# Twenty-five tiles of gathered rows: fetched edge by edge by SyncE instead of by GpSimd

## The chip, the cores and the metric

The kernel runs on one core of a Trainium2 chip. The core has a matrix engine (TensorE, PE in the profile, with its weight loads listed apart as PEld), a vector engine (VectorE, DVE), an activation engine (ScalarE, ACT), a general engine that also issues indirect transfers (GpSimd, POOL), and SyncE (SP), which computes nothing and issues transfers. All of them work through their own list of instructions in order and wait for each other on semaphores. Sixteen DMA engines move the data between the chip's large memory (DRAM below) and the on-chip memory of 128 partitions.

The metric is device time in microseconds of one execution. A comparison takes medians of several executions, and runs of the kernel before made beside those of the kernel after.

## What is computed

A graph of 12,500 nodes and 212,500 edges, of which 12,500 are loops (a node to itself). Every node has 64 numbers. Two layers follow each other, both with a layer norm ahead and a sum onto the nodes at the end:

```python
h = relu(layernorm(x))
# layer 1: a 64x64 matrix for each of 16 edge types
msg = h[src] @ weight[type]
x = x + segment_sum(msg, dst)
h = relu(layernorm(x))
# layer 2: a small network on both ends and 8 attributes of the edge
m = relu(concat(h[src], h[dst], attr) @ W1 + b1) @ W2 + b2
x = x + segment_sum(m, dst)
```

The edges come sorted by dst. src is random, so h[src] is a gather of rows of 64 float32 (256 B) from all over a table.

## The kernel before

The host hands over the arrays with no arithmetic. On the chip the edges that are not loops (200,000 of them) are first compacted into a list edges_c, and then treated in 1563 tiles of 128 edges, in groups of G = 4 tiles, 391 groups for each layer. The list is made in eight parts (UPTO holds their first tiles); the codes and source numbers of part c+1 are computed while part c is worked on.

First layer (`first_layer`, L1249). Per group: `gather` (L1005) has GpSimd issue one indirect DMA for each tile, which lands the 128 rows of h_rows in a buffer `rows` (14 such buffers of a group each, pool `land`, L316). ScalarE builds one-hot codes `oh_r` of target and relation; `products` (L1276) multiplies, on PE, the rows with the codes into `pa`, two matmuls a tile; `add` adds `pa` to a running table on VectorE at a place read from a register. Beside this main line run generators that are advanced by a step with every tile: preparing the next part, compacting and transposing the edge attributes (`attrs`, `turns_of_attrs`, with tiles u_in and u_out), loading h and loop relations of the next block (b_h, b_rel), and finishing blocks of nodes (`finish`, `tail_of`), which ends in the tables a_rows (h times the first part of W1) and b_rows (h times the second part).

Second layer (`second_layer`, L1449). Per group g: GpSimd gathers the rows of a_rows as before; SyncE loads a window of 40 rows of b_rows (`b_win`, two halves, six buffers) from a place that it reads from `first_row` into a register; every fourth group it loads positions (`local_bc`) and attributes (`of_edges`), of which ScalarE makes one-hots. PE multiplies the window with the one-hots into `pz`; one to three groups later VectorE adds the gathered rows, z = pz + rows; ScalarE applies the relu (`hid`), VectorE builds a one-hot `oh`, PE sums over edges (`pa`), and VectorE adds that to `sums`. The landing buffer of group g is free when z has read it.

The order on each engine is the order in which the program writes its instructions: the wrapper `InOrder` (L331 to 348; every operation that goes through it has the line L340 in the profile) holds each engine to it. `windows` (L1027) loads n = RG = 8 numbers of a row on chip into registers of an engine; a place computed from a register goes into a transfer as `bass.ds(r, n)`. A source number of an edge becomes float in `codes` (L939), is transposed on PE and lands as an integer column of `src_c`, from which the gather takes its 128 row numbers:

```python
V.tensor_single_scalar(sf, low, float(N - 1), op=ALU.min)
...
P_.indirect_dma_start(out=t[:, i, :], out_offset=None, in_=table,
    in_offset=bass.IndirectOffsetOnAxis(ap=idx[:, k : k + 1], axis=0))
```

Of the kernel before, what the change touches and what calls it, by code (L numbers as in the profile page):

```python
# [52 lines left out]
P = 128  # L53
N = 12500
D = 64
# [18 lines left out]
G = 4  # L74
# [101 lines left out]


LEAST, MOST = bounds()
WE = W + EA
EARLY = 4  # L180
NBW = 6
# [28 lines left out]
def gnn_kernel(  # L210
# [11 lines left out]
    b_rows = dram.tile([NW, D], F32, name="b_rows")  # L222
    x_mid = dram.tile([NB * P, D], F32, name="x_mid")
    attr_c = dram.tile([EC * EA, 1], F32, name="attr_c")
    attr_l = dram.tile([NB * P * EL, 1], F32, name="attr_l")
    turned_c = dram.tile([NGC * G * EA, P], F32, name="turned_c")
    turned_l = dram.tile([NB * EL, P], F32, name="turned_l")
    src_e = dram.tile([EARLY * 2, 2 * P], I32, name="src_e")
# [84 lines left out]
    def in_order():  # L313
        with ExitStack() as c2:
# [70 lines left out]
            tables = [own.tile([P, RH, SN + AHEAD], F32, name=f"table{k}") for k in range(2)]  # L385
            src_c = own.tile([P, UPTO[-1]], I32, name="src_c")

            rsel = own.tile([P, RH], F32, name="rsel")
            G_.iota(rsel, pattern=[[2, RH]], base=0, channel_multiplier=0, allow_small_or_imprecise_dtypes=True)
            V.tensor_single_scalar(rsel[D:], rsel[D:], 1.0, op=ALU.add)  # L390
# [37 lines left out]
            def weights():  # L428
                for k in range(2):
                    Q_.dma_start(wrel[k * D : (k + 1) * D], w_rel[k::2].rearrange("r i o -> i r o"))  # L430
                    Q_.dma_start(w1ab[k * D : (k + 1) * D], w1[: 2 * D].rearrange("(k i) o -> i k o", k=2))
                    yield
                Q_.dma_start(b1_bc, b1.unsqueeze(0).to_broadcast([P, D]))
                Q_.dma_start(t_loop[N:, :].rearrange("n o -> o n"), none)
                Q_.dma_start(attr_l[N * EL :, :].rearrange("(n c) o -> n (c o)", c=EL), zero[: NB * P - N, :EL])
                for t in hid_l:
                    V_.memset(t[:, :, D:], 1.0)
                yield
                Q_.dma_start(w1c, w1[2 * D :])
# [161 lines left out]
            def loop_attrs(q, psA):  # L601
# [337 lines left out]
            def codes(c, q, row, psA, V, S, T, rest):  # L939
# [16 lines left out]
                V.tensor_single_scalar(low, word, SRC - 1, op=ALU.bitwise_and)  # L956
                V.tensor_single_scalar(rel, word, 14, op=ALU.logical_shift_right)
                yield
                V.tensor_single_scalar(sf, low, float(N - 1), op=ALU.min)
                V.tensor_single_scalar(even, rel, 1, op=ALU.bitwise_and)  # L960
                yield
                V.tensor_tensor(d, q[:n, :, :, 1], bc(first_d, 2, P, [n, 2, P]), op=ALU.subtract)
                V.tensor_tensor(most[:n], d[:, 0, P - 1 :], d[:, 1, P - 1 :], op=ALU.max)
# [38 lines left out]
                    yield  # L1002
                bank.append(1)

            def gather(table, idx, g, last, first=0):  # L1005
                t = land.tile([P, G, D], F32, name="rows")
                tiles = [i for i in range(G) if first <= g * G + i < last]
                for i in tiles:
                    k = g * G + i
                    P_.indirect_dma_start(  # L1010
                        out=t[:, i, :],
                        out_offset=None,
                        in_=table,
                        in_offset=bass.IndirectOffsetOnAxis(ap=idx[:, k : k + 1], axis=0),
                    )
                return t, tiles[-1] + 1
# [232 lines left out]
            def first_layer(psA, loops_0):  # L1249
# [24 lines left out]
                    return g >= RAWG and (g - SHIFT) * G + i < NOT  # L1274

                def products(g, i):  # L1276
                    for half in range(2):
                        T_.matmul(
                            pa_of[g][half * D : (half + 1) * D, i, :],
                            lhsT=rows_of[g][:, i, :],  # L1280
                            rhs=oh_of[g][:, i, half * HW : (half + 1) * HW],
                            start=True,
                            stop=True,
                        )
# [10 lines left out]
                        V_.tensor_tensor(to, to, pa_of[a][:, i, :].rearrange("p (r n) -> p r n", r=RH), op=ALU.add)  # L1295

                at = {}
                behind_ns = [0.0]
                for it in range(NG1 - RAWG + L1_ADD[1]):
                    g = it + RAWG  # L1300
                    if g < NG1:
                        k = (g - SHIFT) * G
                        if it == 0 or k in UPTO:
                            c = sum(k >= b for b in UPTO[1:])
                            for _ in coming:
                                next(fresh, None)
# [3 lines left out]
                        rows_of[g], n_of[g] = gather(h_rows[:, :], src_c, g - SHIFT, NTC, NOT)  # L1310
# [23 lines left out]
                    for j in range(max(len(now), len(adds))):  # L1334
                        for i in range(G):
# [11 lines left out]
                            if it >= BEGIN:  # L1347
# [101 lines left out]
            def second_layer(ps):  # L1449
# [39 lines left out]
                for h in range(2):  # L1489
                    one_hots(0, h)  # L1490
                of_z, of_hid, of_pe, of_add = (turns(lag, NGC) for lag in (L2_Z, L2_HID, L2_PE, L2_ADD))
                for it in range(NGC + L2_ADD[1]):

                    g = it
                    if g < NGC:
                        if g % RG == 0:
                            at_b.update(enumerate(windows(first_row, g, PAD_DST, Q_, min(RG, NGC - g)), g))
                        if g % RB == 0:
                            load_edges(g // RB + 1)
                        a_of[g], n_of[g] = gather((a_early if g < EARLY else a_rows)[:, :], src_c, g, NTC)  # L1500
                        n = n_of[g]
                        if n:
                            bw = b_win[g % NBW]
# [28 lines left out]
                    for g in of_z.get(it, []):  # L1532
                        n = n_of[g]
                        if n:
                            hid_of[g] = wk2.tile([P, G, D], F32, name="z", bufs=3)
                            z, a = (t.rearrange("p (j h) d -> p j h d", h=2) for t in (hid_of[g], a_of.pop(g)))
                            pz_g = pz_of.pop(g)
                            for j, h in ((slice(0, n // 2), slice(0, 2)), (slice(n // 2, n // 2 + 1), slice(0, n % 2))):
                                if n % 2 or h.stop == 2:
# [536 lines left out]
```

## Time and profile before

| | |
|---|---|
| median of 10 runs | 4832.84 us (4828.25 to 4835.29) |
| the profiled execution | 4832.1 us, its span 4830.2 us |
| granted clock of PE | 0.545 of full speed on average |
| GpSimd busy | 2992.2 us, 62% of the span, 3170 instructions |
| PE busy, weight loads busy | 2212.3 us and 1743.4 us, 14955 of each |
| ScalarE busy, VectorE busy | 1636.6 us and 1420.0 us |
| DMA, instructed by GpSimd | 101152 packets, 111.42 MB, 12.8% of 16 engines' span |
| DMA, instructed by SyncE | 454757 packets, 116.50 MB, 11.4% |

How to read it. The profile counts an engine as busy while one of its instructions works; waits, register instructions and the issue of a transfer are not counted for SyncE, so SyncE has no busy time at all and is read from its rows in the timeline. A group of instructions is shown as output<-inputs, the count, busy microseconds, mean nanoseconds of one, and the idle time ahead of them with what ended it; "issue" is idle time for which no wait was found. A view of stretches gives busy time and, in brackets, the number of instructions of an engine within each. In the timeline several like instructions in a row are merged, xN, and the second number is the time from the start of the first to the end of the last.

The chain of work that ended last is here mostly "issue" (37%) and an unknown queue (18%), so it says little about which engine bounds the kernel.

### The profile page before, as it was taken

The page shows a single profiled execution, that of the slowest core. Times are in us where ns is not written, and L with a number is a line of the kernel's source. Part 1 is how long each engine was busy: PE and PEld are TensorE (multiplying, and loading weights), DVE is VectorE, ACT ScalarE, POOL GpSimd, SP SyncE. Part 2 cuts the span into 40 slices and gives each one's busy share as a digit, 9 for nine tenths or more (in the row PEclk, how much of TensorE's full clock was granted, in tenths as well). Part 3 has the DMA queues.
Part 4 walks back from the last instruction along what each step waited for, and adds up shares of the span by engine and source line. Part 5 has one row for each costly group of instructions (what it writes and reads, how often), then busy time and mean ns, then how long its engine had stood idle before and what let it go on. Part 6 is the DMA issues. An engine that isn't in the chain of part 4 may idle for free.

```text
span 4830.2 us, 53034 instructions
## 1 busy us (share of the span) xinstructions
PE 2212.3 (46%) x14955; PEld 1743.4 (36%) x14955; DVE 1420.0 (29%) x4924; ACT 1636.6 (34%) x3341; POOL 2992.2 (62%) x3170
## 2 busy tenths in 40 slices
PE   0334444455543445455445444444444444444445
PEld 0223333333332333333334444444434443444434
DVE  5375564463552333223221111111111111111112
ACT  3444444444443444444432222222222222222222
POOL 5566666666665666666646666666666666666663
PEclk9755555555555555555555555555555555555555
DMA  3222322313323233222211112212121212122111
GB/s 92 54 62 46 67 62 43 68 40 78 67 48 63 49 52 50 45 46 46 47 42 39 41 41 42 43 40 43 40 43 41 43 41 42 41 42 43 40 39 30
DMA packets 569509, 234.60 MB, mean 49 GB/s; under 512 B 455824, under 2 KB 497680, under 8 KB 568950
## 3 DMA queue, kind: packets, MB, share of 16 engines
q0 software_dynamic: 101152, 111.42, 12.8%
q1 hardware_dynamic: 454757, 116.50, 11.4%
q10 hardware_dynamic: 13298, 3.20, 0.3%
q8 instruction: 123, 2.02, 0.2%
q14 instruction: 179, 1.47, 0.1%
HBM read 195.55 MB, written 35.25 MB: 48 GB/s over the span
## 4 chain that ended last, share of the span: by engine, by line
issue 37%; PE 21%; another core or an unknown queue 18%; DVE 7%; ACT 6%; POOL 4%; DMA 2%; DVEq 1%; SPq 1%; ACTq 0%; POOLq 0%
PE pa L340 10%; PE pz L340 5%; POOL rows L340 4%; ACT off_r L340 3%; PE pT L340 2%; DVE table L340 2%; PE po L340 2%; PE hT L340 1%; ACT off L340 1%; DVE z L340 1%; DVE k_a L340 1%; ACT oh_r L340 1%; SPq L340 1%; PE pab L340 1%
## 5 line engine op out<-in xcount | busy, mean ns | idle before, releaser
L340 POOL DMA_INDIRECT rows<-h_rows,src_c x1533 | 1461.9, 954 | 857.7 <-issue 401.8
L340 POOL DMA_INDIRECT rows<-a_rows,src_c x1547 | 1463.8, 946 | 841.0 <-issue 401.8
L340 PE MATMUL pa<-oh_r,rows 128*64 128x96 f32 x6132 | 778.5, 355 | 812.6 <-issue 600.1
L340 PEld LDWEIGHTS pa<-oh_r,rows 128*64 128x64 f32 x6132 | 558.7, 207 | 1044.4 <-issue 952.8
L340 ACT ACTIVATE hid<-z 128x256 f32<-128x256 f32 x391 | 159.8, 411 | 1685.1 <-DVE z L340 1261.3
L340 PE MATMUL pz<-b_win,of_edges 48*128 48x64 f32 x3126 | 497.8, 419 | 409.1 <-issue 366.9
L340 PE MATMUL pa<-oh,hid 128*65 128x40 f32 x3126 | 473.4, 304 | 408.4 <-issue 360.4
L340 DVE TENSOR_TENSOR table<-table,pa 128x96 f32 x1565 | 394.8, 252 | 892.9 <-remote 668.8
L340 PEld LDWEIGHTS pz<-b_win,of_edges 48*128 48x128 f32 x3126 | 425.8, 316 | 488.0 <-issue 428.7
L340 ACT ACTIVATE off_r<-iota_s,code 128x192 bf16<-128x192 f32 x1535 | 570.0, 444 | 0.0
L340 PEld LDWEIGHTS pa<-oh,hid 128*65 128x65 f32 x3126 | 396.6, 221 | 450.1 <-issue 377.8
L340 DVE TENSOR_TENSOR z<-pz,rows 128x256 f32<-128x256 f32 x392 | 164.4, 420 | 1088.0 <-issue 626.7
L340 ACT ACTIVATE oh_r<-off_r 128x768 f32<-128x768 bf16 x392 | 330.3, 843 | 381.1 <-remote 323.4
L340 DVE TENSOR_TENSOR sums<-sums,pa 65x40 f32 x391 | 73.0, 187 | 616.5 <-remote 391.0
L340 PE MATMUL pT<-table,wrel 128*64 128x256 f32 (+1 forms) x800 | 228.4, 579 | 41.8 <-issue 39.9
L340 ACT ACTIVATE off<-local_bc,neg_w 40x1024 bf16<-40x1024 bf16 x196 | 222.5, 1135 | 5.1 <-DMA local_bc<-dst_l 2.4
L340 ACT ACTIVATE of_edges<-off 40x1024 f32<-40x1024 bf16 x196 | 206.2, 1052 | 6.3
L340 DVE SCALAR_TENSOR_TENSOR table<-b_rel,rsel,hT 128x256 f32<-128x256 f32 (+1 forms) x400 | 169.1, 470 | 125.0 <-remote 76.3
L340 DVE COPY_PREDICATED k_a<-move,k_a 128x1712 int32<-128x1712 int32 (+8 forms) x124 | 186.3, 1503 | 2.1 <-issue 0.2
L340 PE MATMUL hT<-ident,b_h 128*64 128x128 f32 x392 | 54.6, 428 | 228.9 <-DVE table L340 79.9
L340 PE MATMUL po<-w2b,sums 65*128 65x64 f32 x196 | 54.0, 329 | 211.6 <-issue 208.3
L340 PE MATMUL po<-w1c,o_at 8*128 8x64 f32 x196 | 56.0, 335 | 194.4 <-issue 180.8
(242 smaller groups left out, 1547.9 us busy)
## 6 DMA issues: line engine op xcount, KB each, us to landing
rows<-a_rows,src_c POOLq DMA_INDIRECT x1547
rows<-h_rows,src_c POOLq DMA_INDIRECT x1533
local_bc<-dst_l SPq DMA_DIRECT2D x194, 80.0 KB
b_win<-b_rows SPq DMA_DIRECT2D x782, 10.0 KB
k_a<-in_attr_k SPq DMA_DIRECT2D x72, 144.0 KB
k_a<-in_attr SPq DMA_DIRECT2D x52, 132.0 KB
u_in<-attr_c SPq DMA_DIRECT2D x97, 64.0 KB
turned_c<-u_out SPq DMA_DIRECT2D x97, 64.0 KB
```

The costliest lines, as they stand in the source:

```text
L340: last_ins[self.engine] = getattr(self.engine, name)(*args, **kw)
```

## The change

Of the tiles, 25 are no longer gathered by GpSimd: the last of four tiles in 14 groups of the first layer (ROWS_1) and in 11 groups of the second (ROWS_2). The source numbers of these tiles are kept as integers and written as rows of a small tile `row_src`, one row of 128 numbers for each. A generator `one_by_one` has SyncE read eight of them at a time into registers and issue one DMA of a single row for each edge, 128 for a tile, into one of two buffers `by_row`; a buffer is used again when the product or the sum that reads it has been written down in the program. In the first layer the generator is advanced one or two steps with each tile (six in a group), in the second four steps in a group, so that a tile takes 22 and 33 groups. `gather` leaves the tile out, `products` and z take the rows from `by_row` instead; z of such a group is made in three instructions.

With it go some smaller edits: the register loads of the second layer read four places at a time and not eight (for SyncE's window of b_rows and VectorE's place in sums), the source numbers are clipped as integers and converted by an instruction of their own, and the table attr_l is longer by 60 rows, with the limit of a store moved to match.

```diff
+ROWS_1 = [UPTO[c] // G + k for c in range(1, PARTS) for k in (25, 47) if UPTO[c] // G + k < NGC - 1]
+ROWS_2 = list(range(40, NGC - 8, 33))
+ROWS = [g * G + G - 1 for g in ROWS_1 + ROWS_2]
...
-    attr_l = dram.tile([NB * P * EL, 1], F32, name="attr_l")
+    attr_l = dram.tile([(NB * P + KLN) * EL, 1], F32, name="attr_l")
...
+            row_src = own.tile([len(ROWS), P], I32, name="row_src")
+            by_row = [own.tile([P, D], F32, name=f"by_row{k}") for k in range(2)]
+            known = set()
...
-                Q_.dma_start(attr_l[N * EL :, :].rearrange("(n c) o -> n (c o)", c=EL), zero[: NB * P - N, :EL])
+                Q_.dma_start(attr_l[N * EL :, :].rearrange("(n c) o -> n (c o)", c=EL), zero[: NB * P + KLN - N, :EL])
...
-                V_.tensor_single_scalar(to, firsts, float(NB * P - KLN), op=ALU.min)
+                V_.tensor_single_scalar(to, firsts, float(NB * P), op=ALU.min)
...
-                V.tensor_single_scalar(sf, low, float(N - 1), op=ALU.min)
+                V.tensor_single_scalar(low, low, float(N - 1), op=ALU.min)
+                V.tensor_copy(sf, low)
                 V.tensor_single_scalar(even, rel, 1, op=ALU.bitwise_and)
+                for m, k in enumerate(ROWS):
+                    if b0 <= k < b0 + nt:
+                        r, i = divmod(k - b0, 2)
+                        (Q_ if c else nc.sync).dma_start(row_src[m : m + 1, :], low[r : r + 1, i, :])
+                        known.add(m)
...
+            def one_by_one(table, of, at):
+                for m in range(at, at + len(of)):
+                    while m not in known or (m - at >= 2 and of[m - at - 2] not in used):
+                        yield
+                    t = by_row[m % 2]
+                    for e0 in range(0, P, RG):
+                        for e, r in enumerate(windows(row_src[m : m + 1], e0, N - 1, Q_), e0):
+                            Q_.dma_start(t[e : e + 1, :], table[bass.ds(r, 1), :])
+                            yield
+                    fetched[of[m - at]] = t
+                    yield
...
-            def gather(table, idx, g, last, first=0):
+            def gather(table, idx, g, last, first=0, but=()):
...
-                for i in tiles:
+                for i in tiles[: G - 1] if g in but else tiles:
...
                 def products(g, i):
+                    r = rows_of[g][:, i, :]
+                    if i == G - 1 and g >= RAWG and g - SHIFT in ROWS_1:
+                        while g - SHIFT not in fetched:
+                            next(by_rows)
+                        r = fetched.pop(g - SHIFT)
+                        used.add(g - SHIFT)
...
-                            lhsT=rows_of[g][:, i, :],
+                            lhsT=r,
...
+                by_rows = one_by_one(h_rows, ROWS_1, 0)
...
+                            if it >= BEGIN:
+                                for _ in range(1 + i % 2):
+                                    next(by_rows, None)
...
+                used.clear()
+                by_rows = one_by_one(a_rows, ROWS_2, len(ROWS_1))
...
+                    if g >= 6:
+                        for _ in range(G):
+                            next(by_rows, None)
...
-                        if g % RG == 0:
-                            at_b.update(enumerate(windows(first_row, g, PAD_DST, Q_, min(RG, NGC - g)), g))
+                        if g % RB == 0:
+                            at_b.update(enumerate(windows(first_row, g, PAD_DST, Q_, min(RB, NGC - g)), g))
...
+                            m = n - 1 if g in ROWS_2 else n
...
+                            if g in ROWS_2:
+                                assert n == G
+                                V_.tensor_tensor(z[:, 1, 1, :], pz_g[:, 1, 1, :], fetched.pop(g), op=ALU.add)
+                                used.add(g)
...
-                            if g % RG == 0:
-                                at.update(enumerate(windows(place_row, g, SN + AHEAD2 - W, V_, min(RG, NGC - g)), g))
+                            if g % RB == 0:
+                                at.update(enumerate(windows(place_row, g, SN + AHEAD2 - W, V_, min(RB, NGC - g)), g))
```

More of the change, by code (lines that the diff above doesn't have):

```diff
@@ L1003, in take @@
                 bank.append(1)
-            def gather(table, idx, g, last, first=0):
+            def one_by_one(table, of, at):
[9 more added lines that the diff above has]
+                    yield
+            fetched, used = {}, set()
+            def gather(table, idx, g, last, first=0, but=()):
                 t = land.tile([P, G, D], F32, name="rows")
                 tiles = [i for i in range(G) if first <= g * G + i < last]
-                for i in tiles:
+                for i in tiles[: G - 1] if g in but else tiles:
                     k = g * G + i
@@ L1309, in first_layer @@
                             coming = beside_part(c, psA)
-                        rows_of[g], n_of[g] = gather(h_rows[:, :], src_c, g - SHIFT, NTC, NOT)
+                        rows_of[g], n_of[g] = gather(h_rows[:, :], src_c, g - SHIFT, NTC, NOT, ROWS_1)
                     for g in of_oh.get(it, []):
@@ L1491, in second_layer @@
                 of_z, of_hid, of_pe, of_add = (turns(lag, NGC) for lag in (L2_Z, L2_HID, L2_PE, L2_ADD))
+                used.clear()
+                by_rows = one_by_one(a_rows, ROWS_2, len(ROWS_1))
                 for it in range(NGC + L2_ADD[1]):
                     g = it
+                    if g >= 6:
+                        for _ in range(G):
+                            next(by_rows, None)
                     if g < NGC:
-                        if g % RG == 0:
-                            at_b.update(enumerate(windows(first_row, g, PAD_DST, Q_, min(RG, NGC - g)), g))
+                        if g % RB == 0:
+                            at_b.update(enumerate(windows(first_row, g, PAD_DST, Q_, min(RB, NGC - g)), g))
                         if g % RB == 0:
                             load_edges(g // RB + 1)
-                        a_of[g], n_of[g] = gather((a_early if g < EARLY else a_rows)[:, :], src_c, g, NTC)
+                        a_of[g], n_of[g] = gather((a_early if g < EARLY else a_rows)[:, :], src_c, g, NTC, 0, ROWS_2)
                         n = n_of[g]
@@ L1537, in second_layer @@
                             pz_g = pz_of.pop(g)
-                            for j, h in ((slice(0, n // 2), slice(0, 2)), (slice(n // 2, n // 2 + 1), slice(0, n % 2))):
-                                if n % 2 or h.stop == 2:
+                            m = n - 1 if g in ROWS_2 else n
+                            for j, h in ((slice(0, m // 2), slice(0, 2)), (slice(m // 2, m // 2 + 1), slice(0, m % 2))):
+                                if m % 2 or h.stop == 2:
                                     V_.tensor_tensor(*(t[:, j, h, :] for t in (z, pz_g, a)), op=ALU.add)
+                            if g in ROWS_2:
+                                assert n == G
+                                V_.tensor_tensor(z[:, 1, 1, :], pz_g[:, 1, 1, :], fetched.pop(g), op=ALU.add)
+                                used.add(g)
                     for g in of_hid.get(it, []):
```

## The prediction

> **What bounds the kernel now.** I read the page's busy line and its costliest groups first, then GpSimd's waits, then stretches of the timeline in the second layer, and last SyncE's own rows, because SyncE is the engine that takes the work over.
>
> The page: GpSimd is the busiest engine, and nearly all of it are two groups of gathers, 1533 from h_rows and 1547 from a_rows (16 more read a_early).
>
> ```profile
> PE 2212.3 (46%) x14955; PEld 1743.4 (36%) x14955; DVE 1420.0 (29%) x4924; ACT 1636.6 (34%) x3341; POOL 2992.2 (62%) x3170
> ...
> L340 POOL DMA_INDIRECT rows<-h_rows,src_c x1533 | 1461.9, 954 | 857.7 <-issue 401.8
> L340 POOL DMA_INDIRECT rows<-a_rows,src_c x1547 | 1463.8, 946 | 841.0 <-issue 401.8
> ```
>
> One gather is 0.95 us and 0.30 us of gap, 1.25 us. By the list of instructions by tile the first layer's gathers run from 82.5 to 2418 us and the second's from 2455 to 4779, so one gather passes in 2335/1533 = 1.52 us and in 2324/1563 = 1.49 us. The quarter of a microsecond above 1.25 is waiting. GpSimd's waits from 2600 to 4600 us say for whom:
>
> ```profile
> POOL rows L340 <- issue: 352.1, 1153, 0.6
> POOL rows L340 <- DVE oh L340: 330.2, 83, 4.3
> ```
>
> Every 4 groups, 4.0 us long, GpSimd waits until VectorE's z has freed a landing buffer 14 groups back. So GpSimd is not alone the bound; the consumers hold it. But the consumers are fast when GpSimd is quiet. The busy time in six stretches, PE's weight loads alone (columns: stretch and length, busy us and count, granted clock, DMA share, GB/s):
>
> ```profile
> 3502.00:3514.60 12.60, 1.70 (x6) 0.50 0.23 42
> 3514.60:3522.60 8.00, 6.83 (x56) 0.50 0.29 67
> 3522.60:3538.40 15.80, 2.46 (x12) 0.50 0.16 30
> 3538.40:3546.60 8.20, 7.07 (x60) 0.50 0.20 44
> ...
> 4779.50:4824.00 44.50, 29.09 (x222) 0.50 0.07 17
> ```
>
> GpSimd is idle from 3511.6 to 3515.6. In the 8 us from just before its restart PE gets 56 weight loads through, in the 15.8 us after them 12, one step of about 0.7 us at a time, until GpSimd has again stood still for some 2 us. The clock is 0.50 throughout. After the last gather (4779) PE stays quick and a group passes in about 3.2 us against 5.94 before. So while gathers run without a break PE falls into a slow stretch, which ends only when GpSimd is held up. SyncE falls into it with PE, as its timeline shows:
>
> ```profile
> 3540.48 1.75 SPq L340 DMA_DIRECT2D b_win<-b_rows  x4
> ...
> 3516.19 10.05 SPq L340 DMA_DIRECT2D b_win<-b_rows  x8
> ...
> 4800.11 3.92 SPq L340 DMA_DIRECT2D b_win<-b_rows  x8
> ```
>
> These are DMAs from a place held in a register, the form that the change adds: 0.44 and 0.49 us each in a quick stretch, 1.26 us on average in the ten microseconds where a slow stretch begins. It is not all waiting for data: the register move ahead of each takes 29 ns in the median and up to 1395 ns (instructions of b_win).
>
> ```profile
> L340 SPq MOVE b_win<-b_rows x782: 2/29/1395, 2480.6 to 4803.7; - x196
> ...
> L1029 SPq TENSOR_LOAD <-first_row x49: 762/784/1193, 2479.6 to 4785.1; - x49
> ```
>
> **What the change removes.** 25 gathers on GpSimd, 14 and 11. At 1.25 us (GpSimd alone) that is 31 us, at the pace at which gathers really pass 14 x 1.52 + 11 x 1.49 = 38 us. I take 38: one gather less lets GpSimd stop sooner, and the slow stretch end sooner.
>
> **What it adds on SyncE.** 25 x 128 = 3200 DMAs of 256 B and 25 x 16 = 400 loads of eight registers. In quick stretches: 0.50 us a DMA and 0.79/8 = 0.10 us of load, 0.60 us an edge, 77 us a tile, 1920 us in all. In slow stretches the price lies between 1.26 and 2.1 us (register step, move and DMA, each 0.7); I take 1.5 us, nearer the measured average, a third of the quick speed. A one-row transfer from a register's place is not in this trace: the nearest are b_win's 40 rows (0.50 us with its register steps) and the one-row load of place_row (0.70 us, no register); I take b_win's, the same form, and 0.70 would fill the first layer to 5.5 of 6.0 us. They stand in SyncE's queue in front of everything that it issues later: in the first layer h and relations for the next block, u_in, x_mid, a_rows, b_rows; in the second b_win, edges and one-hot places, which PE needs.
>
> First layer, 6.0 us a group, 6 edges in each: 3.6 us, beside what SyncE issues now: by the list of DMA issues u_in, turned_c, b_rel, b_h, x_b, x_mid, a_early, a_rows, b_rows and k_a, 704 at 0.40 us = 282 us over 389 groups, 0.7 us. Sum 4.3 of 6.0. Second layer, 5.94 us, 4 edges: 2.4 us, beside 782 b_win x 0.50 + 583 others x 0.32 + 98 loads x 0.79 = 655 us, 1.7 us a group. Sum 4.1 of 5.94. If SyncE were always quick, all of it would be hidden, and the 38 us gained.
>
> It isn't always quick. Second layer, a cycle of 4 groups, 23.7 us, of which 8.2 are quick: needed 4 x 4.1 = 16.4 us of quick work, to be had 8.2 + 15.5/3 = 13.4. Short 3.0 us. SyncE then gets later from cycle to cycle, b_win comes late, z after it, GpSimd waits longer, and that wait is quick time: a microsecond more of idle gives itself, and puts the next slow stretch off by some 1.6 us (idle 4.0 us here, next onset some 6.5 us after the restart, on average over the cycles from 3000 to 3500 us), worth 1 + 1.6 x 2/3 = 2.1 us. So the cycle grows by about 1.4 us; the 11 tiles are fetched over 11 x 33 groups, 91 cycles: +130 us. First layer, 2 groups, 11.8 us: around 1840 us GpSimd stands still 2.1 us in each and PE is quick for some 4.2 us (its weight loads, over the cycles from 1800 to 2000 us). Needed 8.6, to be had 4.2 + 7.6/3 = 6.7, short 1.9, an idle microsecond worth 1.9: +1.0 us for each of 14 x 22/2 = 154 pairs: +150 us.
>
> Ends of this term: nothing at all (quick stretches suffice, the 38 us stand), and SyncE's work done in quick time only: an idle of I gives I less the 2.2 us until PE is quick again, and 1.6 I after it, so (I - 2.2) + 1.6 I = 16.4, I = 7.2, 3.2 us more than now x 91 = 290 us, and in the first layer (0.9 us and 1.4) (I - 0.9) + 1.4 I = 8.6, I = 4.0, 1.9 us x 154 = 290 us, together 580. I take 280, between them, since SyncE does move in slow stretches.
>
> **Small edits.** Where SyncE begins a buffer again it waits for the product or sum that read it last, 23 times; behind it stand b_win or h loads that are issued 3 to 6 groups ahead, so nothing. The second layer's register loads are of 4, not 8: 49 more at 0.79 us on SyncE (counted in the 1.7) and 49 more on VectorE at 0.6 us = 29 us, and 11 z in three pieces instead of one, some 0.5 us each: VectorE is idle 85% of that layer, hidden except where z is what GpSimd waits for, at most 10 us. A conversion more in codes, 7 at 0.3 us, one more small DMA a fetched tile, 25 at 0.7 us, and a somewhat larger fill of zeros: in VectorE's and SyncE's slack.
>
> **A rule against it.** The trace: SyncE's register DMAs follow each other at 0.44 us, and their waits for earlier b_win DMAs are 39 us in all, 1.5 us at the longest. The Trainium skill, "DMA: Bandwidth & Descriptors", section "Rules for kernel authors", says that many small transfers should be joined into a large one and that under 64 KB one pays mostly overhead; the section "Anatomy of one DMA" puts about 2.0 us of fixed time on each (its fit is for GpSimd's). At 2.0 us one after the other the 3200 would be 6400 us, an estimate from that page; the spacing of 0.44 us shows that they overlap, so the issue price is the one to use.
>
> **Sum.** The profiled execution took 4832.1 us (span 4830.2 and 1.9 around it), 0.7 us under the median of 4832.84. 4832 - 38 + 280 = about 5075 us.
>
> **Rivals.**
> 1. It does what it says, faster: 4833 - 38 = 4795. For it: 4.3 of 6.0 and 4.1 of 5.94 us in quick time, SyncE now waits for others for half of the first layer (494 us for ACT's u_out from 300 to 2300 us), and buffers let it run ahead. It decides as long as SyncE's price per edge stays below about 0.9 us on average, where 6 edges and 0.7 us fill a group of the first layer. Against it: 15 of 23.7 us are slow.
> 2. SyncE gets hardly anything done in slow stretches, or its 10,000 more instructions (three a DMA, and the loads) and 3200 landings lengthen them: 4795 + 580 = 5375, beyond if the slow stretches grow. Against: counted in the trace from 3000 to 3500 us, quick parts with some 21 SyncE instructions last 7.2 to 8.3 us and those with some 30 last 8.1 to 9.4; more instructions did not end them sooner.
> 3. Gain and loss cancel: 4833. It needs a loss of 38 us, about 0.15 us in each of the 245 cycles and pairs.
>
> **Chances.** The forecast (SyncE late, 4880 to 5280) 0.52; rival 2 with more than that 0.21; rival 1, with smaller losses included, 0.20; rival 3 0.07. What a measurement of this kernel can tell from no change is about 0.2%, 10 us. So faster 0.20, same 0.06, slower 0.74. The range goes from the full gain, 4793, to the end of the forecast's term, 5375; what lies outside is the worse half of rival 2. The forecast's own range is 4880 to 5280.
>
> **What would show it.** 3055 gathers instead of 3080, the same 0.95 us each. by_row DMAs on SyncE at 0.45 to 0.5 us in quick and above 1.2 us in slow stretches, SyncE without long waits while they run. GpSimd's waits for VectorE longer than 4.0 us per cycle in the second layer, and than 2.1 us in the first; groups longer while tiles are fetched and as before in the last 20 groups, where nothing is. Wrong it would be if slow stretches last as long with SyncE never late (rival 1), or if a landing, not the issue, holds SyncE.

## The result and the profile after

The kernel after took 5304.5 us (median of 8 runs, 5289.92 to 5313.61), the kernel before beside it 4833.0 us. The ratio is 1.0973, 95% interval 1.0963 to 1.0982: 471 us slower, where 242 slower was forecast and 5280 us was the upper end of the forecast's own range. The profiled execution of the kernel after took 5300.15 us, its span is 5298.3.

The experiments were run on three chips, and the kernel before itself took other times there: about 3967 us on two of them, 4789 and 4838 us on the third. Each comparison below is with the kernel before, run beside it on the same chip. I call a chip late or prompt by that time, since it decides the sign of the result: on a prompt chip the change makes the kernel 0.8% faster. Which chip the first result came from isn't on record; its 4833 us make it a late one. The third chip was late both times, the other two were met once each, so whether lateness is a chip's own or a condition that it was in is not shown.

The page of the kernel after, on the late chip of the first result (columns: busy us and mean ns of one, then idle us before them and what ended most of it):

```profile
PE 2183.1 (41%) x14955; PEld 1751.7 (33%) x14955; DVE 1422.2 (27%) x4954; ACT 1643.7 (31%) x3341; POOL 2954.1 (56%) x3145
...
L343 POOL DMA_INDIRECT rows<-h_rows,src_c x1519 | 1438.6, 947 | 1086.9 <-issue 391.7
L343 POOL DMA_INDIRECT rows<-a_rows,src_c x1536 | 1449.1, 943 | 1065.1 <-DVE oh L343 571.8
L343 PE MATMUL pz<-b_win,of_edges 48*128 48x64 f32 x3126 | 623.6, 433 | 1296.8 <-DMA b_win<-b_rows 989.7
```

The gathers are 25 fewer and each as long as before. What grew is the idle time ahead of them, and ahead of `pz` the wait for `b_win`, a load that SyncE issues. By the list of instructions by tile the first layer's gathers now run from 82.1 to 2677.1 us and the second's from 2713.7 to 5247.6: 259.5 and 209.4 us longer than before, together 468.9 us, where the span grew by 468.1. GpSimd's waits from 2800 to 4800 us, as long a stretch of the second layer as the one shown of before (columns: us in all, times, longest):

```profile
POOL rows L343 <- DVE oh L343: 469.4, 135, 7.7
POOL rows L343 <- issue: 312.3, 1024, 0.3
POOL rows L343 <- DVE z L343: 66.1, 15, 15.0
```

The wait for VectorE grew from 330.2 to 469.4 us and is now up to 7.7 us long instead of 4.3. PE's weight loads from 3400 to 3600 us and after the last gather, kernel after (columns: stretch and length, busy us and count, granted clock, DMA share, GB/s):

```profile
3400.00:3600.00 200.00, 81.00 (x544) 0.50 0.18 38
5247.60:5292.00 44.40, 29.12 (x222) 0.50 0.07 17
```

Before, the same 200 us held 598:

```profile
3400.00:3600.00 200.00, 83.02 (x598) 0.50 0.20 42
```

The clock and the tail after the last gather (222 loads, 29.1 us, in both) are unchanged. SyncE's rows come from the list of instructions of `by_row`, then that of `row_src` (columns: count, shortest/median/longest ns, first and last start), and then its timeline from 1000 to 1012 us (columns: start, length, and how many in a row):

```profile
L343 SPq MOVE by_row<-h_rows x1792: 1/29/1408, 303.8 to 2595.2; - x200
L343 SPq DMA_DIRECT2D by_row<-h_rows x1792: 1/228/2542, 304.1 to 2596.0; - x200
```

```profile
L1056 SPq TENSOR_LOAD <-row_src x400: 1/709/3331, 302.9 to 5112.6; - x134
```

```profile
1000.06 11.96 SPq L343 DMA_DIRECT2D by_row<-h_rows  x11
```

A register move takes 29 ns in the median and up to 1408. Eleven edges in a row take 11.96 us, and that is hardly waiting for others: SyncE's longest sum of waits for one cause is 34.3 us in the whole span, where before it waited 531.8 us for ScalarE's `u_out` alone. The row of before, then that of the kernel after (columns: us in all, times, longest):

```profile
SPq L340 <- ACT u_out L340: 531.8, 62, 61.0
```

```profile
SPq L343 <- DMA by_row<-h_rows: 34.3, 71, 1.3
```

Two measures taken from the instruction rows serve for all runs below. The price of an edge is the time from the start of SyncE's DMA ahead of it to the start of its own, distances of 8 us or more left out. In the kernel after it is 1.02 us in the first layer and 1.04 us in the second on average: half of the edges (52 and 53%) are under 0.75 us, with a mean of 0.46, and the other half have a mean of 1.61 and 1.71 us. Nearly every edge with a register load ahead of it, one in eight, is in that other half; on a prompt chip all of these are above 0.75 us too, 1.43 and 1.34 us on average. Of the edges without a load 41 and 40% are above 0.75 us here, with the same means of 1.61 and 1.71, and on a prompt chip 8 and 1%. A late step is a distance of 0.67 to 0.745 us between the starts of two successive instructions of one engine, counted over 1800 us of the second layer (1600 on a prompt chip): SyncE of the kernel before has 642 among 2847 instructions.

### The profile page after: what moved, and what is told of

It is laid out like the page before. It is cut to its first block, busy times and chain, and to the rows that moved or that the text cites. A ratio compares the mean times of both kernels' runs of the same rounds, so it can differ in the third digit from the quotient of the medians.

```text
span 5298.3 us, 63235 instructions
## 1 busy us (share of the span) xinstructions
PE 2183.1 (41%) x14955; PEld 1751.7 (33%) x14955; DVE 1422.2 (27%) x4954; ACT 1643.7 (31%) x3341; POOL 2954.1 (56%) x3145
## 3 DMA queue, kind: packets, MB, share of 16 engines
q1 hardware_dynamic: 462019, 117.35, 10.5%
## 5 line engine op out<-in xcount | busy, mean ns | idle before, releaser
L343 POOL DMA_INDIRECT rows<-h_rows,src_c x1519 | 1438.6, 947 | 1086.9 <-issue 391.7
L343 PE MATMUL pz<-b_win,of_edges 48*128 48x64 f32 x3126 | 623.6, 433 | 1296.8 <-DMA b_win<-b_rows 989.7
L343 PE MATMUL pa<-oh_r,rows 128*64 128x96 f32 x6076 | 667.1, 351 | 844.8 <-issue 461.5
L343 PEld LDWEIGHTS pz<-b_win,of_edges 48*128 48x128 f32 x3126 | 519.6, 315 | 1398.6 <-DMA b_win<-b_rows 920.0
L343 PEld LDWEIGHTS pa<-oh_r,rows 128*64 128x64 f32 x6076 | 513.1, 207 | 1012.4 <-issue 867.7
L343 PE MATMUL pa<-oh,hid 128*65 128x40 f32 x3126 | 430.7, 311 | 57.7 <-issue 30.2
L343 ACT ACTIVATE oh_r<-off_r 128x768 f32<-128x768 bf16 x392 | 330.2, 842 | 252.3 <-remote 196.9
L343 PEld LDWEIGHTS pa<-oh,hid 128*65 128x65 f32 x3126 | 373.5, 226 | 104.0 <-issue 31.8
L343 DVE TENSOR_TENSOR z<-pz,rows 128x256 f32<-128x256 f32 (+2 forms) x403 | 164.4, 411 | 744.5 <-PE pz L343 419.6
L343 PE MATMUL hT<-ident,u_in 128*128 128x128 f32 (+3 forms) x107 | 44.5, 416 | 334.9 <-DMA u_in<-attr_c 131.4
L343 ACT COPY table<-table 128x1024 f32<-128x1024 f32 x49 | 51.2, 1045 | 306.3 <-DVE table L343 236.1
```

Of the source, the lines that this page charges most:

```text
L343: last_ins[self.engine] = getattr(self.engine, name)(*args, **kw)
```

## Experiments

**The first four runs met a chip without late steps.** There the kernel before takes 3967.83 us. The first run leaves the 25 gathers out, the second keeps them all and fetches the rows beside them unread, the third puts constants in place of the register, the fourth gives the work to ScalarE.

```diff
 # a_no_fetch
-                        while g - SHIFT not in fetched:
-                            next(by_rows)
-                        r = fetched.pop(g - SHIFT)
+                        r = rows_of[g][:, G - 2, :]
...
-                by_rows = one_by_one(h_rows, ROWS_1, 0)
+                by_rows = iter(())
...
 # b_fetch_beside
-                for i in tiles[: G - 1] if g in but else tiles:
+                for i in tiles:
...
-                        r = fetched.pop(g - SHIFT)
+                        fetched.pop(g - SHIFT)
...
 # c_constant
-                        for e, r in enumerate(windows(row_src[m : m + 1], e0, N - 1, Q_), e0):
-                            Q_.dma_start(t[e : e + 1, :], table[bass.ds(r, 1), :])
+                        for e, r in enumerate([(97 * (m * P + e)) % N for e in range(e0, e0 + RG)], e0):
+                            Q_.dma_start(t[e : e + 1, :], table[r : r + 1, :])
 # d_act
-                        for e, r in enumerate(windows(row_src[m : m + 1], e0, N - 1, Q_), e0):
-                            Q_.dma_start(t[e : e + 1, :], table[bass.ds(r, 1), :])
+                        for e, r in enumerate(windows(row_src[m : m + 1], e0, N - 1, S_), e0):
+                            S_.dma_start(t[e : e + 1, :], table[bass.ds(r, 1), :])
```

> The kernel after without the 3200 fetches: the 25 gathers are left out and nothing takes their place; products and z of those tiles use the rows of the tile before, so the values of 25 of 3126 tiles are not computed from their own rows. It measures the gain by itself. Theory (one gather less lets GpSimd stop sooner): 38 us less than before, 4785 to 4805. Rival (the consumers hold GpSimd, so a gather less is only a longer wait): 4833, as before.

> The kernel after with all 3105 of before's gathers in these two loops kept as well: SyncE fetches the 25 tiles beside them and nobody reads what it fetches. Theory (SyncE's own time makes b_win, u_in and the rest late): as slow as the kernel after plus the gathers, 5300 to 5345. Rival (the loss comes from PE and VectorE waiting for rows that arrive late): about 4835 to 4870.

> The kernel after with constant sources in place of registers (a fixed row for every edge, so these 25 tiles get the wrong rows): the same 3200 DMAs of one row, but one instruction on SyncE instead of three, and no register loads. Theory (SyncE's instruction time): an edge costs about 0.33 us quick and 0.7 us slow instead of 0.60 and 1.5 to 2.1; the second layer's cycle then needs 16 x 0.33 + 6.8 = 12.1 us of quick work where 13.4 are to be had, so most of the loss goes: 4795 to 4900. Rival (the landings or the transfers of 3200 small DMAs hold it): 5200 to 5300.

> The kernel after with the 400 register loads and 3200 DMAs issued by ScalarE instead of SyncE, at the same places of the program. Theory (PE and SyncE have slow stretches, ScalarE does not: its out DMA took 0.38 us in the middle of one, its activations their usual time): second layer ScalarE is busy 25% of the time and gets 2.4 us more of each 5.94, it fits and gains 16 us; first layer it is busy 43% and gets 3.6 us more of each 6.0, full, so up to 100 us lost there: 4800 to 4930. Rival (a slow stretch strikes whatever engine issues many instructions, or the DMAs themselves are the cost): 5150 to 5350.

Measured, with the ratio to the kernel before: a_no_fetch 3936.04 us, 0.9921 (0.9904 to 0.9938); b_fetch_beside 3968.19, 1.000 (0.999 to 1.001); c_constant 3936.37, 0.9921 (0.9905 to 0.9938); d_act 3953.87, 0.9966 (0.9951 to 0.998). So 25 gathers are worth 31.8 us there, 1.27 us each, and 3200 fetches on SyncE cost nothing that can be measured. On ScalarE they take back 18 us; in its trace a store of GpSimd waits 15.1 us for a landing of `by_row`, and 395 us of ScalarE's idle time ahead of `off_r` are put down to such landings; which of these makes the 18 us is not shown. These runs did not test what makes the first result slow, because what I took for its cause is missing: in the trace of b_fetch_beside SyncE has 4 late steps, its register moves for `by_row` never exceed 39 ns, and GpSimd waits more than 0.5 us only five times.

**The change again, and more loads for each edge.** These runs met a late chip, kernel before 4837.91 us. The expectations of the last two were written for a prompt one.

```diff
 # i_load_each (j_load_two: 2 in place of 1)
-                    for e0 in range(0, P, RG):
-                        for e, r in enumerate(windows(row_src[m : m + 1], e0, N - 1, Q_), e0):
+                    for e0 in range(0, P, 1):
+                        for e, r in enumerate(windows(row_src[m : m + 1], e0, N - 1, Q_, 1), e0):
```

> The change as it is, beside the kernel before on one chip. The last runs were on a chip where the kernel before takes 3967.83 us, its gathers pass at 1.27 us without a wait, and both the full fetch beside all gathers (3968.19 us) and constants in place of the gathers (3936.37 us) showed no cost of SyncE's. Theory (SyncE's price of an edge decides, and only where its steps are slowed does it exceed the group's time): on such a chip 25 gathers of 1.26 us go and nothing comes back, 3936 us, ratio 0.992. On a chip where the kernel before takes 4833 us: 5300 us, ratio 1.097. Rival (what the change costs lies in the sources in registers or in the small edits, which the constants did not have together): above 3968 us on either chip.

> One register load for each edge in place of one for eight: SyncE's price of an edge goes from 0.40 us (a run of eight took 3.19 us) to about 0.3 + 0.8 = 1.1 us (a load took 0.79 us). Where gathers pass without a wait a group takes 5.0 us. Theory (SyncE's price decides): in layer 1 a group brings 6 edges, 6 x 1.15 + 0.7 of its other issues = 7.6 us, over 5.0 by 2.6 us in 308 groups, +800 us; in layer 2 4 x 1.15 + 1.7 = 6.3 us, over by 1.3 us in 363 groups, +470 us; with the 32 us of the gathers off about 5200 us where the kernel before takes 3968. GpSimd then waits on VectorE's and TensorE's buffers as it does after the change on the chip of the first result. Rival (SyncE was never what was late; the slow steps of TensorE are): no change against the change as it is, about 3936 us.

> One register load for two edges: SyncE's price of an edge about 0.3 + 0.8/2 = 0.7 us. Theory: layer 1 6 x 0.7 + 0.7 = 4.9 us of a group of 5.0, layer 2 4 x 0.7 + 1.7 = 4.5 us: just within, 3936 to 4000 us where the kernel before takes 3968, and a steep step from here to one load for each edge. Rival (SyncE's work costs in proportion, not past a point): a third of what one load for each edge costs, some 4300 us.

Measured: the change 5289.29 us, 1.0933 (1.0915 to 1.0951); a load for two edges 5762.41, 1.191 (1.189 to 1.193); a load for each 6136.46, 1.2693 (1.2672 to 1.2715). Nothing but SyncE's loads differs between the three. The gathers on the page of the change, then on that of i_load_each, show who waits:

```profile
L343 POOL DMA_INDIRECT rows<-h_rows,src_c x1519 | 1437.8, 947 | 1087.9 <-issue 389.7
L343 POOL DMA_INDIRECT rows<-a_rows,src_c x1536 | 1449.0, 943 | 1066.5 <-DVE oh L343 573.6
```

```profile
L343 POOL DMA_INDIRECT rows<-h_rows,src_c x1519 | 1441.2, 949 | 1515.7 <-PE pa L343 826.7
L343 POOL DMA_INDIRECT rows<-a_rows,src_c x1536 | 1452.7, 946 | 1412.5 <-DVE oh L343 901.5
```

GpSimd's idle time rises by 428 and 346 us over that of the change, and it waits for PE's products and for VectorE, not for SyncE itself. The price of an edge goes from 1.02 to 1.20 and 1.32 us in the first layer and from 1.04 to 1.18 and 1.26 in the second. If SyncE is the bound while tiles are fetched, each step in price must come out as a step in time, times 6 edges and 308 groups or 4 edges and 363 groups. That gives 327 and 225 us in the first layer and 195 and 113 in the second, 860 in all; the layers grew by 280, 193, 194 and 156 us, 823 in all. SyncE's longest sum of waits for one cause is 58.2 us in i_load_each, so the price is the time of its own instructions and not a wait for others. So SyncE's price is the time here, and the rival of i_load_each, that SyncE was never late, falls on this chip. The rival of j_load_two expected a third of what a load for each edge costs; it is 473 of 847 us, and of the price 0.16 of 0.26 us.

**The parts of the cost.** The constant sources, ScalarE and the missing gathers were run once more, again on a late chip, kernel before 4788.76 us, with the same edits as above.

> Constant sources, so that an edge is one DMA of SyncE, without the register's write and the loads (it computes with other rows than the reference's), on a chip where the kernel before takes 4838 us; where it takes 3968 this gave 3936. The change costs some 490 us net there. Theory (SyncE's instructions for an edge, each about 0.7 us while GpSimd gathers without a break, are what is late): an edge goes from 3.1 instructions to 1, its quick price from 0.60 to 0.25 us; by the prediction's own cycles layer 2 needs 16.4 - 16 x 0.35 = 10.8 us of quick work where 13.4 are to be had, layer 1 8.6 - 12 x 0.35 = 4.4 of 6.7: SyncE is not late, 4800 us (4790 to 4880). Rival (it is the 3200 DMAs, their count or what they put on the DMA engines): 5250 us or more.

> The change with ScalarE issuing the edges in place of SyncE, registers and loads as they are, on a chip where the kernel before takes 4838 us; where it takes 3968 this gave 3954. Theory (the slow steps are TensorE's and SyncE's; no row shows ScalarE slowed): ScalarE's edges stay at some 0.4 us, 6 of them and 2.1 us of its other work in a group of 6.0 us, so it is not late: 25 x 1.5 us off and the one wait of some 15 us for a landing, 4800 to 4830 us. Rival (every engine's register and DMA instructions are slowed while GpSimd gathers): ScalarE is late as SyncE was, 5200 us or more, since ScalarE's own work waits behind it.

> The 25 gathers left out and nothing in their place (those 25 tiles are computed from rows that nobody fetched), on a chip where the kernel before takes 4838 us; where it takes 3968 it took 31.8 us off. Theory (what a gather takes off is the mean pace that gathers pass at, 1.5 us, since the waits of 4 us come back every so many groups): 38 us off, 4800 us. Rival (a gather takes off its own 1.25 us alone): 31 us off, 4807 us. Second rival (with less to do GpSimd stands still longer and the others catch up): within 5 us of before.

Measured: c2_constant 4819.51 us, 1.0055 (1.0038 to 1.0072); d2_act 4882.56, 1.0183 (1.0164 to 1.0203); a2_no_fetch 4749.88, 0.9917 (0.99 to 0.9933). The missing gathers bring 38.9 us, 1.56 us each: the pace of the gathers, as the first theory had it, though the interval of the ratio, 32 to 48 us, shuts out the rival's 31 us only just. Over that kernel the fetches cost 70 us as bare DMAs. By the ratio of the change, 1.0933 to 1.0973, they cost 486 to 506 us of 4789 with register moves and loads. So some 420 to 440 us, six sevenths, come with the instructions that reach the source through a register (the register step, the move and the share of a load), and not with the 3200 transfers or their landings. The rival falls. The theory expected no cost at all from the bare DMAs, though, and that was too little; the gathers of the first layer take 21 us longer than without the fetches and those of the second 48 us (2316 against 2295 us, 2333 against 2285). In the second PE waits for `b_win`, by the waits of the run:

```profile
PE pz L343 <- DMA b_win<-b_rows: 477.2, 251, 5.6
```

Without the fetches (a2_no_fetch) the list has no such row for `pz`.

ScalarE costs 133 us over the missing gathers, more than expected but about a quarter of what the same work costs on SyncE (492 us, see the table below). The loads, moves and DMAs are the same in both, so what they cost depends on the queue that they stand in. The same kernel's moves on the prompt chip, and then here:

```profile
L343 ACTq MOVE by_row<-h_rows x1792: 29/29/29, 183.4 to 1855.5; - x200
```

```profile
L343 ACTq MOVE by_row<-h_rows x1792: 2/29/1525, 301.1 to 2364.6; - x200
```

ScalarE has 494 late steps here and 1 on the prompt chip. So late steps aren't SyncE's own: they come to ScalarE as soon as it issues such instructions, against the theory that I wrote for this run.

**Half of it, and the change on a prompt chip.** Half the tiles at half the rate, and the change a third time. They met another prompt chip, kernel before 3966.59 us.

```diff
-ROWS_1 = [UPTO[c] // G + k for c in range(1, PARTS) for k in (25, 47) if UPTO[c] // G + k < NGC - 1]
-ROWS_2 = list(range(40, NGC - 8, 33))
+ROWS_1 = [UPTO[c] // G + k for c in range(1, PARTS) for k in (47,) if UPTO[c] // G + k < NGC - 1]
+ROWS_2 = list(range(73, NGC - 8, 66))
...
-                                for _ in range(1 + i % 2):
+                                for _ in range(1 if i < 3 else 0):
...
-                        for _ in range(G):
+                        for _ in range(G // 2):
```

> Half the tiles (7 of the first layer, 5 of the second) fetched at half the rate, 2 edges a step in place of 4 in layer 2 and 3 a group on average in place of 6 in layer 1; 12 gathers go. Where the kernel before takes 4789 to 4838 us the whole change costs some 490 us on SyncE and brings 39. Theory of the prediction (SyncE is late only past the quick time it has to spare): layer 1 needs 12 x 0.60 / 2 + 1.4 = 5.0 us in two groups where 6.7 are to be had, layer 2 16 x 0.60 / 2 + 6.8 = 11.6 us in four where 13.4 are: SyncE is not late and 12 x 1.5 = 18 us go, ratio 0.996. Rival (SyncE's work costs without a threshold, in proportion to its instructions): half of 490 comes and 18 us go, +225 us, ratio 1.047. Between them: by the constant sources, which cost 70 us with two fifths of the quick work, 70 to 130 us come, ratio 1.011 to 1.023. Where the kernel before takes 3968 us: 12 x 1.26 = 15 us off, ratio 0.996.

> The change as it is, beside the half of it on the same chip. Theory (what it costs is SyncE's lateness, and that comes from the slow steps that the chip of the kernel before shows or does not show): on a chip where the kernel before takes 3968 us, 3936, ratio 0.992; where it takes 4789 to 4838, 5240 to 5300, ratio 1.093 to 1.097. Rival (the loads and registers cost on any chip): over 1.0 where the kernel before takes 3968.

Measured: the half 3952.3 us, 0.9965 (0.9952 to 0.9977); the change 3934.5 us, 0.9919 (0.9903 to 0.9936). The change takes 32.1 us off and the half 14.3, 1.28 and 1.19 us a gather, about the 1.27 us that a_no_fetch gave on the other prompt chip: the removed gathers and nothing else. The rival, that loads and registers cost on any chip, falls. Whether half the rate would have been free on a late chip wasn't tried. SyncE's rows of the change on this chip, by the same lists and the same microseconds of the timeline as above:

```profile
L343 SPq MOVE by_row<-h_rows x1792: 29/29/39, 184.2 to 1838.5; - x200
L343 SPq DMA_DIRECT2D by_row<-h_rows x1792: 219/228/2513, 184.3 to 1838.6; - x200
```

```profile
L1056 SPq TENSOR_LOAD <-row_src x400: 704/792/1523, 183.3 to 3738.8; - x134
```

```profile
1000.13 2.29 SPq L343 DMA_DIRECT2D by_row<-h_rows  x6
1002.53 0.36 SPq L343 DMA_DIRECT2D turned_c<-u_out  x1
```

Here six edges take 2.29 us, and SyncE then turns to its other work. GpSimd's waits in that run:

```profile
POOL rows L343 <- issue: 789.6, 2590, 0.3
POOL rows L343 <- DMA rows<-a_rows,src_c: 68.3, 224, 0.3
```

Hardly anything is left but the 0.3 us between gathers, so GpSimd alone sets the pace: its gathers of the second layer take 1939 us, 4.96 us for each of the 391 groups, and SyncE's 0.61 us an edge in the first layer and 0.59 in the second fit beneath it.

The four prices side by side, on late chips, with the cost of the fetches over the missing gathers (ratio less 0.9917, times the kernel before that was run beside it; the 0.9917 is that of a2_no_fetch, which ran beside c2_constant):

| | price of an edge, layers 1 and 2 | cost |
|---|---|---|
| c2_constant | 0.50, 0.49 us | 66 us |
| the change (after_again) | 1.02, 1.04 us | 492 us |
| j_load_two | 1.20, 1.18 us | 964 us |
| i_load_each | 1.32, 1.26 us | 1343 us |

The first is 66 by ratios and 70 by medians. Between the first two rows a microsecond more per edge costs some 800 us, past them some 3300 us, about the 3200 edges themselves: the cost begins gently below one microsecond and then counts in full. No version was found that is faster than the kernel before on both kinds of chip: on a late one only the kernel without the rows was.

## Why the prediction was right, and where it was off

The direction and the mechanism, SyncE late by its own instructions, were right for the chip that was measured, and the time fell into the full range. It lies above the forecast's own range of 4880 to 5280 us, though, where the prediction put rival 2 at a chance of 0.21. Of that rival's reasons two are not borne out: SyncE does get work done in slow stretches, at 1.61 and 1.71 us an edge, and the 3200 landings come with the bare DMAs too, which cost 66 to 70 us. Whether the added instructions lengthen the slow stretches, its third, isn't separated from a term that was too small, see below. And the forecast holds for a late chip, on which its trace was taken and the result measured. It doesn't say so: on a prompt one even its sign would have been wrong. Point by point:

- *"I take 38"* for the 25 gathers: 38.9 us measured on a late chip. The lower bound of 31 us is what they are worth on a prompt one, 31.8 and 32.1, where GpSimd waits for nothing.
- *0.60 us an edge in quick stretches*: 0.61 and 0.59 us on a prompt chip. *"I take 1.5 us"* in slow ones: the edges without a load that are above 0.75 us have a mean of 1.61 and 1.71.
- *+130 and +150 us for SyncE being late, 280 of a possible 580*: this is the term that was mis-sized. The layers grew by 259.5 and 209.4 us; with the gathers that went (14 x 1.52 = 21 and 11 x 1.49 = 16 us) that is 281 and 226 us, 507 in all, near the upper end, at which SyncE's work is done in quick time only. The forecast cycles imply a mean price: 12.8 us for 8.6 us of quick work is 0.89 us an edge in the first layer, 25.1 for 16.4 is 0.92 in the second. Measured were 1.02 and 1.04. That difference over 1792 and 1408 edges is some 400 us, more than the 227 us that are missing, so it is enough to carry the miss. Which half of the cycle's working made it too low can be counted in the trace, as an accounting and not an experiment. By the forecast cycles 6.6 of 8.6 us and 11.8 of 16.4 us of SyncE's work, 77 and 72%, pass in quick time; of the edges without a load only 59 and 60% are under 0.75 us. With the measured prices (0.47 and 1.61 us in the first layer, 0.46 and 1.71 in the second, 1.58 and 1.69 with a load) the forecast's shares would have given 0.84 and 0.92 us an edge, so the prices were near enough. What was too large is the share of quick time. Whether idle time of GpSimd brings less of it than was taken, or SyncE's added instructions lengthen the slow stretches, isn't shown.
- *Rival 1, decided by a price below about 0.9 us an edge*: on the late chips the price was above it and the change lost, on the prompt chips below it and the change gained 32 us. As an edge it was too sharp: the constant sources, at 0.50 us, still cost 66 to 70 us, though by the cycles SyncE had time to spare. That quick time to spare on average isn't there at the moment when `b_win` has to be issued would fit PE's wait for `b_win` in that run, but it is only argued.
- *The small edits at about nothing*: the kernels without the gathers and without fetches contain them. They gained 31.8 us on a prompt chip, where 25 x 1.25 is 31, and 38.9 on a late one, where 38 was counted, so nothing is left for the edits to have cost.
- *"if a landing, not the issue, holds SyncE"*: not so; SyncE's waits for `by_row` DMAs are 34.3 and 27.0 us in all. The 2.0 us of fixed time in the Trainium skill's "DMA: Bandwidth & Descriptors", section "Anatomy of one DMA", would have made 6400 us, an estimate; on a prompt chip SyncE's distances for 3167 of the 3200 edges add up to 1898 us (the others are over 8 us and left out), and on the late one the mean distance is 1.02 and 1.04 us, so on neither does such a fixed time set SyncE's pace.
- *What would show it*: 3055 gathers of 0.95 us and SyncE without long waits are as written. GpSimd waits for VectorE more than 4.0 us in each cycle of four groups, 6.1 us (469.4 us in 2000 us, a cycle being 25.9 us on average now), but in more waits, 135 against 83, and one alone takes 3.5 us on average, up to 7.7. From 5130 to 5247.6 us, with nothing left to fetch, 76 gathers start; before, 76 started in the same time ahead of the end of the gathers. So the groups outside the fetched stretch are as they were.

What the prediction did not see is that its bound goes with the chip. It read the late steps in the trace as a part of this program; with them gone the same change does what rival 1 said.

## What to carry to other kernels

Work that moves to an idle queue is priced by that queue's time for an instruction while the kernel runs, and one that reaches its place through a register has three instructions and not one: 0.60 us an edge where instructions come promptly, over 1.0 where they don't. If the engine that takes it over issues the loads of the others too, ask what it must issue in time, and not only how long it is idle. And a profile in which several engines move one instruction at a time, with no wait named, should be taken on a second chip before a change is judged by it.

## What was unexpected of the hardware

The same program takes 4789 to 4838 us on one chip and 3966.6 to 3967.8 us on two others, at about the same granted clock (0.545 in the kernel before's trace, 0.535 in the trace of the change on a prompt chip, 0.50 in the second layer of either). On the late chip successive instructions start 0.67 to 0.745 us apart very often. Counted as said above: SyncE 642 in the kernel before, 672 without the fetches, 909 with them; on prompt chips 4 and 6. PE's weight loads have 208 in the kernel before, 327 without the fetches and 9 in the kernel after, where it waits for `b_win` instead; without the fetches on a prompt chip they have 3. GpSimd and VectorE have none that stand out (12 and 1 in the kernel before).

What makes the steps late stays open. The trace of before ties them to gathers without a break, since they end when GpSimd stands still; but on the prompt chips GpSimd gathers without any break and they don't come. So the gathers alone are not the cause. Nor do the traces show slower transfers: in the kernel after the packets of SyncE's queue take 10.5% of 16 engines' span of 5298.3 us on the late chip and 14.1% of that of 3931.3 us on a prompt one, about 8900 us in both, and the packets that bring instructions 256 and 251 us. No run here took away anything else that could be the cause.
